# The first four batches of a two-layer graph kernel: loads by other queues, statistics two by two, and two products swapped

## The chip, the cores and the metric

The kernel runs on one core of a Trainium2 chip. The metric is the device time of one execution in microseconds (us). Before the change the median of three runs is 1966.01 us (1965.82 to 1967.39). A core has engines that run side by side, each through its own queue in program order: TensorE (PE, matmuls; PEld in a profile is its loading of the stationary operand), VectorE (DVE), ScalarE (ACT), GpSimd (POOL) and SyncE (SP, here only to issue DMAs). They meet at semaphores.

## The reference

Inputs are x of 128 batches x 128 nodes x 512 features, an adjacency matrix `adj` of 128 x 128, and the weights of one attention layer, all float32. Cut to what matters:

```python
# layer 0: W1 and W2 are both adj, so C - A is the bias b alone
A   = einsum('od,bdn->bon', adj, x)
pre = A[:, :, None, :] + b[None, :, None, None]
x   = layernorm(x + max(relu(pre), axis=-1))      # a single maximum per row of A
# layer 1: masked attention with 8 heads, a projection, its layernorm added
q, k, v = x @ w_qkv
o  = softmax(where(adj == 0, -inf, q @ k.T / 8)) @ v
o  = o @ w_proj + b_proj
x  = layernorm(x + o + layernorm(o) * ln_gamma + ln_beta)
```

So layer 0 needs, for each batch, one 128x128 by 128x512 product with `adj`, the maximum of each of its rows, plus bias, not below zero, added to that row of x, and a layernorm over the 512 features.

## The kernel before

Batches are worked in groups of four. x is loaded in pairs of batches (`load(q)`, lines 103 to 111), either one DMA of 512 KB on SP's queue, or one of 256 KB for each batch on the queues that are given.

A batch f of layer 0 goes through these steps, each a function:

- `l0_mm` (line 282): TensorE multiplies `adjT` with x into a PSUM tile `pa`. A float32 matmul is two instructions.
- `l0_max` (line 286): VectorE takes the row maximum `amax` (line 288) and makes `r` of it with the bias (line 290).
- `l0_add` (line 292): ScalarE adds `r` to x (line 293).
- `bn` (line 247): VectorE takes the statistics (line 249) and aggregates them into a column of `mv` (line 250).
- `finish_stats` (line 252): for all columns of one `mv`, VectorE negates the mean (line 259), and GpSimd adds epsilon (line 261), raises to the power -1/2 and multiplies (line 77). `stats` (line 635) is `bn` for several batches and `finish_stats` behind them.
- `l0_norm` (line 295): ScalarE scales and shifts x (line 275).
- `l0_transpose_pe` (line 314), for the first group only: TensorE transposes x by four 128x128 pieces (line 318), and VectorE copies the result into `x1T` (line 320). Batches f and f + 1 of a pair fill the halves that later products read as one operand of 256 columns.

The products of layer 1 with weights are done by a scheme with seven products in place of eight (`Unit`, lines 163 to 196). A unit works on four batches and a slice of weights. Its products have numbers: `product(1)` and `product(2)` read the first pair's `x1T` and unchanged weights; `product(4)` reads the second pair's `x1T`; products 5, 6, 7 and 3 read sums of the pairs (`left_sums`, made here by VectorE, `run_sums(sums, nc.vector)` on line 708). Products 4, 5, 6, 7 read sums of the weights, which `weight_sums` (line 124) makes on GpSimd: four subtractions for 256 columns. The third and fourth of these depend on the ones before, and product 4 reads the fourth. A product is 8 matmul instructions of 256 columns. Products 1, 6 and 7 share PSUM bank 1; after 1, after 6 and after 7 ScalarE copies that bank to SBUF (`snap`, line 185); 5 and 3 share bank 3.

`keep_warm(n)` (line 85) issues n matmuls of zeros (two instructions each) into a tile that nobody reads.

The order of every engine's instructions is the order in which the program text calls these functions (each is pinned in program order). At the start it is: the adjacency matrix and the bias on SP; pairs 0 and 1 of x, the first batch of each pair on ACT's queue and the second on SP's (lines 137 and 138); a broadcast of beta on ACT; the first 256 columns of the query and key weights by four DMAs on SP, pair 2, the other 256 columns, pair 3. Then the stretch that the diff touches, lines 677 to 716: the four `l0_mm`; for each batch maximum, add and statistics; one `finish_stats` for batches 0 and 1 and one for 2 and 3; both halves of the weight sums; the four norms; ten keep-warm matmuls; the transposes of batches 0 and 1; two keep-warm matmuls. Then unit `cur` begins: product 1, the transposes of batches 2 and 3, product 2, the sums of x, the beta additions and spills of pairs 0 and 1 (GpSimd and SP), products 4, 6 and 5. Batches 4 to 7 of layer 0 follow (`pa` again), and from then on a loop over pairs of batches runs to the end.

Of the kernel before, what the change touches and what calls it, by code (L numbers as in the profile page):

```python
# [9 lines left out]
F32 = mybir.dt.float32  # L10
AF = mybir.ActivationFunctionType
ALU = mybir.AluOpType
# [4 lines left out]
def kernel(  # L17
# [30 lines left out]
    nc = tc.nc  # L48
    B, P, D = x.shape
# [3 lines left out]
    G = 4  # L53
    GT = G * P
    HT = GT // 2
    HE = D // 2
# [10 lines left out]
    small = ctx.enter_context(tc.tile_pool(name="small", bufs=4))  # L67
# [5 lines left out]
    def pe(*args, **kwargs):  # L73
        pin(nc.tensor.matmul(*args, **kwargs))  # L74

    def tt(eng, dst, a, b, op):
        pin(eng.tensor_tensor(dst, a, b, op))  # L77
# [7 lines left out]
    def keep_warm(n):  # L85
        for _ in range(n):
            pe(idle, lhsT=zeros[:, :P], rhs=zeros, start=True, stop=True)
# [6 lines left out]
    def broadcast(queue, name, src):  # L94
        t = const.tile([P, D], F32, name=name)
        pin(queue.dma_start(out=t, in_=src.partition_broadcast(P)))
        return t
# [3 lines left out]
    xs, pairs = {}, {}  # L101

    def load(q, *queues):
        tag, bufs = ("o", 3) if 2 <= q <= 4 else ("x", 2)
        pairs[q] = t = sb.tile([P, 2, D], F32, tag=tag, name=f"x_{q}", bufs=bufs)
        for j, queue in enumerate(queues):
            pin(queue.dma_start(out=t[:, j], in_=x[2 * q + j]))
        if not queues:
            pin(nc.sync.dma_start(out=t, in_=x[ds(2 * q, 2)].rearrange("j p d -> p j d")))
        for j in range(2):  # L110
            xs[2 * q + j] = t[:, j]
# [9 lines left out]
                )  # L121
            )

    def weight_sums(w, cols, width):
        t = w[:, :, :, ds(cols, width)]
        b11, b21, b22, b12 = (t[:, i] for i in range(4))
        tt(nc.gpsimd, t[:, 4], b12, b11, ALU.subtract)
        tt(nc.gpsimd, t[:, 6], b22, b12, ALU.subtract)
        tt(nc.gpsimd, t[:, 5], b22, t[:, 4], ALU.subtract)
        tt(nc.gpsimd, t[:, 3], b21, t[:, 5], ALU.subtract)  # L130

    WQK = [P, 7, 2, D]
    wqk = sb.tile(WQK, F32, tag="wqk", name="wqk")
    wv = const.tile([P, 7, 2, HE], F32, name="wv")
    wp = const.tile([P, 7, 2, HE], F32, name="wp")

    for q in range(2):
        load(q, nc.scalar, nc.sync)
    be_bc = broadcast(nc.scalar, "be_bc", ln_beta)
    weight_load(wqk, w_qkv, 0, D, 0, HE)  # L140
    load(2)
# [102 lines left out]
    NC = 6  # L244
    stat_of = {}

    def bn(src, mv, k):
        st = small.tile([P, 6], F32, tag="st", name=f"st_{k}_{mv.name}")
        pin(nc.vector.bn_stats(st, src))
        pin(nc.vector.bn_aggr(mv[:, k], st))  # L250

    def finish_stats(mv, keys, eng=None, fused=0):

        n = len(keys)
        if n == 0:
            return
        sh = small.tile([P, NC], F32, tag="sh", name=f"sh_{mv.name}")
        if eng is None:
            pin(nc.vector.tensor_scalar(sh[:, :n], mv[:, :n, 0], -1.0, None, ALU.mult))
        rs = small.tile([P, NC], F32, tag="rs", name=f"rs_{mv.name}")  # L260
        pin(nc.gpsimd.tensor_scalar(rs[:, :n], mv[:, :n, 1], EPS, None, ALU.add))  # L261
        tt(nc.gpsimd, rs[:, :n], rs[:, :n], mhalf.to_broadcast([P, n]), ALU.pow)
        if eng is None:
            tt(nc.gpsimd, sh[:, :n], sh[:, :n], rs[:, :n], ALU.mult)
        elif n > fused:

            part = slice(fused, n)
            pin(eng.tensor_scalar(sh[:, part], mv[:, part, 0], -1.0, None, ALU.mult))
            tt(eng, sh[:, part], sh[:, part], rs[:, part], ALU.mult)
        for k, key in enumerate(keys):  # L270
            stat_of[key] = rs[:, k : k + 1], sh[:, k : k + 1]

    def normalize(dst, src, key):
        rs, sh = stat_of.pop(key)
        pin(nc.scalar.activation(dst, src, AF.Identity, bias=sh, scale=rs))  # L275
# [6 lines left out]
    def l0_mm(f, tag="pa"):  # L282
        pas[f] = psum.tile([P, D], F32, tag=tag, name=f"pa_{f}")
        pe(pas[f], lhsT=adjT, rhs=xs[f], start=True, stop=True)

    def l0_max(f):
        amax = small.tile([P, 1], F32, tag="amax", name=f"amax_{f}")
        pin(nc.vector.tensor_reduce(amax, pas.pop(f), AX.X, ALU.max))
        rr[f] = small.tile([P, 1], F32, tag="r", name=f"r_{f}")
        pin(nc.vector.tensor_scalar(rr[f], amax, bias0, 0.0, ALU.add, ALU.max))  # L290

    def l0_add(f):
        pin(nc.scalar.activation(xs[f], xs[f], AF.Identity, bias=rr.pop(f)))

    def l0_norm(f):
        normalize(xs[f], xs[f], ("y", f))

    def x1T_tile(g):
        if g not in x1T:
            x1T[g] = sb.tile([P, 2, KC, 2, Q, QS], F32, tag="x1T", name=f"x1T_{g}", bufs=2)  # L300
        return x1T[g]
# [12 lines left out]
    def l0_transpose_pe(f):  # L314
        g, h, j = place(f)
        ps = psum.tile([P, KC, P], F32, tag=f"pss{j % 2}", name=f"pt_{f}")
        for c in range(KC):
            pin(nc.tensor.transpose(ps[:, c], xs[f][:, ts(c, P)], ident))
        pin(
            nc.vector.tensor_copy(x1T_tile(g)[:, h, :, j].rearrange("p c i b -> p c (i b)"), ps)  # L320
        )
# [35 lines left out]
    def x_sums(g):  # L357
        t = x1T[g].rearrange("p h c j i b -> p h c (j i b)")
        blocks = [t[:, h, ds(2 * d, 2)] for h in range(2) for d in range(2)]
        x_lefts[g], sums = left_sums(f"x_{g}", *blocks)  # L360
        return sums

    def qk_unit(g, q):
        for h in range(2):
            qk[g, q, h] = sb.tile(
                [P, 2, 2, HT], F32, tag=f"qk{h}", name=f"qk_{g}_{q}_{h}", bufs=2 + h
            )
        out = {(h, c): qk[g, q, h][:, c] for h in range(2) for c in range(2)}
        return Unit(f"qk_{g}_{q}", x_lefts[g], weight_stationary(wqk, 2 * q * P), out)
# [13 lines left out]
    def place(b):  # L383
        g, j = divmod(b, G)
        return g, j // 2, j % 2
# [111 lines left out]
    def o_sums(g):  # L497
        blocks = [oT[g, h][:, ds(2 * d, 2)] for h in range(2) for d in range(2)]
        o_lefts[g], sums = left_sums(f"o_{g}", *blocks)
        return sums  # L500
# [134 lines left out]
    def stats(name, *items, eng=None, fused=0):  # L635

        mv = small.tile([P, NC, 2], F32, tag="mv", name=f"mv_{name}")
        for k, (kind, b) in enumerate(items):
            bn({"o": o_of, "z": zs.get, "y": xs.get}[kind](b), mv, k)
        finish_stats(mv, items, eng, fused)  # L640
        return mv
# [33 lines left out]


    for f, tag in enumerate(("pa", "po", "b3", "b4")):
        l0_mm(f, tag)
    mv = [small.tile([P, NC, 2], F32, tag="mv", name=f"mv_first_{k}") for k in range(2)]
    for f in range(G):  # L680
        l0_max(f)
        l0_add(f)
        if f > 0:
            bn(xs[f - 1], mv[(f - 1) // 2], (f - 1) % 2)
        if f == 2:
            finish_stats(mv[0], [("y", 0), ("y", 1)])
    bn(xs[3], mv[1], 1)
    finish_stats(mv[1], [("y", 2), ("y", 3)])
    weight_sums(wqk, 0, HE)
    weight_sums(wqk, HE, HE)  # L690
    for f in range(G):
        l0_norm(f)
    keep_warm(10)
    for f in range(2):
        l0_transpose_pe(f)
    keep_warm(2)


    sums = x_sums(0)
    cur = qk_unit(0, 0)  # L700
# [10 lines left out]
        l0_spill(q)  # L711
    cur.result(0, 0)
    cur.product(4)
    cur.product(6)
    cur.snap(2)
    cur.product(5)
    for f, tag in zip(range(G, 2 * G), ("pa", "po", "pss0", "pss1")):
        l0_mm(f, tag)
    for f in range(G, 2 * G):
# [6 lines left out]
    cur = qk_unit(0, 1)  # L726
# [3 lines left out]
    bp_bc = broadcast(nc.sync, "bp_bc", b_proj)  # L730
    stats("second", *(("y", f) for f in range(G, 2 * G)))
    weight_sums(wv, 0, HE)
    before.snap(3)
    before.result(1, 1)
# [36 lines left out]
    for p in range(LAST + 1):  # L771
# [4 lines left out]
        f = p + 5 if p + 5 < B // 2 else None  # L776
        ta, tb, to = tails(p)
        mv = small.tile([P, NC, 2], F32, tag="mv", name=f"mv_{p}")
# [22 lines left out]
        if ph == 0 and g > 0:  # L801
            sums = o_sums(g - 1)
# [262 lines left out]
    mv = small.tile([P, NC, 2], F32, tag="mv", name="mv_last_4")  # L1065
# [19 lines left out]
    mv = small.tile([P, NC, 2], F32, tag="mv", name="mv_last_5")  # L1085
# [11 lines left out]
    mv = small.tile([P, NC, 2], F32, tag="mv", name="mv_last_6")  # L1097
# [11 lines left out]
    mv = small.tile([P, NC, 2], F32, tag="mv", name="mv_last_7")  # L1109
# [9 lines left out]
    mv = small.tile([P, NC, 2], F32, tag="mv", name="mv_last_8")  # L1119
# [8 lines left out]
    mv = small.tile([P, NC, 2], F32, tag="mv", name="mv_last_9")  # L1128
# [48 lines left out]
```

## Time and profile before

| | us |
|---|---|
| median of three runs | 1966.01 (1965.82 to 1967.39) |
| the profiled execution | 1967.67 |
| its span, first to last instruction | 1965.7 |
| TensorE busy in the span | 1936.3 (99%) |
| VectorE, ScalarE, GpSimd busy | 1560.8, 1062.2, 1296.1 |
| mean granted clock of TensorE | 0.995 |
| first matmul of product 1 starts at | 18.88 |
| first matmul of batch 4 of layer 0 starts at | 29.44 |

Times inside a profile count from the start of the span. A row of the timeline gives start, busy time, engine, line of the program, operation, the tiles written and read, and in brackets how long the engine had been idle and what ended that. Rows that follow one another on an engine are merged, so a row can hold many instructions (x8). Matmuls overlap: a single one takes longer in the row than the distance to the next. "Clock" is the share of TensorE's full speed that was granted.

### The profile page before, as it was taken

The numbers are of one execution on the slowest core, as the hardware profiler recorded it, in microseconds if no ns is written. First come the engines' busy times: TensorE is split into PE (matmuls) and PEld (weight loads), VectorE is DVE, ScalarE is ACT, GpSimd is POOL, SyncE is SP. The second block draws the span as 40 slices with busy tenths as digits, with TensorE's granted clock in tenths as the row PEclk, the third lists the DMA queues.
The fourth block names the chain that finished last, engine by engine and source line by source line (L and its number), as shares of the span: only waits on it lengthen the run. The fifth ranks groups of instructions, "written<-read, shape, count | busy, mean of one in ns | idle before, by whom it ended". The sixth has DMA issues, their size and how long they took to land.

```text
span 1965.7 us, 33048 instructions
## 1 busy us (share of the span) xinstructions
PE 1936.3 (99%) x11543; PEld 1639.7 (83%) x11543; DVE 1560.8 (79%) x2512; ACT 1062.2 (54%) x3084; POOL 1296.1 (66%) x824
## 2 busy tenths in 40 slices
PE   9999999999999999999999999999999999999995
PEld 6888888888888888888888888888888888888883
DVE  6767878778778788787787787887887877877876
ACT  3444655555545546555555455465565555554565
POOL 6336666767667677667676676676676766676748
PEclk9999999999999999999999999999999999999998
DMA  6747576576576676675765755766757667667554
GB/s 216 164 131 182 145 188 173 161 204 162 166 198 160 174 193 159 185 180 161 196 169 164 203 155 169 197 159 180 190 156 191 168 168 201 160 167 199 135 186 141
DMA packets 445654, 341.75 MB, mean 174 GB/s; under 512 B 276912, under 2 KB 378416, under 8 KB 445488
## 3 DMA queue, kind: packets, MB, share of 16 engines
q1 hardware_dynamic: 445056, 338.85, 64.2%
q8 instruction: 92, 1.51, 0.3%
q10 hardware_dynamic: 432, 0.79, 0.1%
q14 instruction: 74, 0.61, 0.1%
HBM read 172.82 MB, written 166.72 MB: 173 GB/s over the span
## 4 chain that ended last, share of the span: by engine, by line
PE 95%; DVE 2%; POOL 1%; DMA 1%; ACT 0%; issue 0%; SPq 0%; POOLq 0%; ACTq 0%; DVEq 0%
PE b_qk L74 39%; PE b_v L74 19%; PE b_o L74 18%; PE pss L74 6%; PE po L74 6%; PE pa L74 6%; POOL zl L77 1%; DMA x<-in_x_dram 0%; DMA wlast<-spill 0%; DVE s L77 0%; POOL rs_mv_last L77 0%; PE idle L74 0%; DVE pu L442 0%; DMA out_dram<-xr 0%; DVE s L402 0%
## 5 line engine op out<-in xcount | busy, mean ns | idle before, releaser
L74 PE MATMUL b_qk<-s_x,wqk 128*128 128x256 f32 x2048 | 473.3, 379 | 1.0 <-DVE s_x L77 0.7
L74 PEld LDWEIGHTS b_qk<-s_x,wqk 128*128 128x128 f32 x2048 | 388.9, 190 | 55.2 <-issue 1.3
L421 ACT ACTIVATE s<-s,nmax 128x128 f32<-128x128 f32 x1024 | 396.1, 391 | 5.7 <-DVE nmax L414 5.7
L74 PE MATMUL b_qk<-x1T,wqk 128*128 128x256 f32 x1536 | 358.7, 383 | 0.1
L74 PEld LDWEIGHTS b_qk<-x1T,wqk 128*128 128x128 f32 x1536 | 286.7, 190 | 45.1 <-issue 1.0
L77 POOL TENSOR_TENSOR z<-z,ga_bc 128x1024 f32<-128x1024 f32 x58 | 164.5, 2836 | 169.3 <-ACT z L275 169.3
L261 POOL TENSOR_SCALAR rs_mv<-mv 128x6 f32<-128x6 f32 (+2 forms) x61 | 14.6, 239 | 381.3 <-DVE mv L250 381.3
L77 DVE TENSOR_TENSOR s<-s,rec 128x1024 f32<-128x1024 f32 x128 | 251.7, 1967 | 4.4
L187 ACT COPY u_qk<-b_qk 128x512 f32<-128x512 f32 x192 | 112.5, 586 | 246.4 <-PE b_qk L74 245.2
L74 PE MATMUL b_v<-wv,s_x 128*128 128x256 f32 x1024 | 236.9, 379 | 0.0
L74 PE MATMUL b_o<-wp,s_o 128*128 128x256 f32 x992 | 231.2, 381 | 3.3 <-POOL s_o L77 2.3
L74 PEld LDWEIGHTS b_v<-wv,s_x 128*128 128x128 f32 x1024 | 194.4, 190 | 26.6
L74 PEld LDWEIGHTS b_o<-wp,s_o 128*128 128x128 f32 x992 | 189.2, 191 | 30.6 <-POOL s_o L77 2.7
L193 DVE TENSOR_TENSOR qk<-b_qk,u_qk 128x512 f32<-128x512 f32 x256 | 168.0, 675 | 57.1 <-PE b_qk L74 44.8
L402 DVE SCALAR_TENSOR_TENSOR s<-pss,mask 128x512 f32<-128x512 f32 x256 | 164.1, 683 | 59.0 <-PE pss L74 58.8
L77 POOL TENSOR_TENSOR x<-x,be_bc 128x1024 f32<-128x1024 f32 x64 | 181.9, 2843 | 33.5 <-DVE rec L432 27.4
L193 DVE TENSOR_TENSOR v<-b_v,u_v 128x512 f32<-128x512 f32 x128 | 87.0, 680 | 137.4 <-PE po L74 132.5
L421 ACT ACTIVATION_READ_ACCUMULATOR s<-s,nmax 128x1 f32 x1024 | 194.4, 190 | 0.0
L187 ACT COPY u_v<-b_v 128x512 f32<-128x512 f32 x96 | 56.2, 586 | 236.7 <-PE b_v L74 236.7
L187 ACT COPY u_o<-b_o 128x512 f32<-128x512 f32 x93 | 54.4, 585 | 237.7 <-PE b_o L74 237.7
L74 PE MATMUL b_v<-wv,x1T 128*128 128x256 f32 x768 | 176.2, 379 | 0.0
L74 PEld LDWEIGHTS b_v<-wv,x1T 128*128 128x128 f32 x768 | 145.9, 190 | 32.2 <-issue 13.9
(121 smaller groups left out, 3396.7 us busy)
## 6 DMA issues: line engine op xcount, KB each, us to landing
hop<-pu SPq DMA_DIRECT2D x128, 512.0 KB, 3.4
pT<-hop SPq DMA_DIRECT2D x512, 128.0 KB, 3.6
spill<-x SPq DMA_DIRECT2D x64, 512.0 KB, 4.8
x<-in_x_dram SPq DMA_DIRECT2D x62, 512.0 KB, 4.3
xhop<-xt SPq DMA_DIRECT2D x248, 128.0 KB, 2.3
x1T<-xhop SPq DMA_DIRECT2D x248, 128.0 KB, 3.9
xr<-spill SPq DMA_DIRECT2D x59, 512.0 KB, 3.2
out_dram<-xr SPq DMA_DIRECT2D x58, 512.0 KB, 4.1
```

Of the source, the lines that this page charges most:

```text
L74: pin(nc.tensor.matmul(*args, **kwargs))
L77: pin(eng.tensor_tensor(dst, a, b, op))
L187: pin(nc.scalar.copy(t, self.banks[1]))
L193: nc.vector.tensor_tensor(self.out[half, col], self.banks[bank], self.snaps[k], ALU.add)
L261: pin(nc.gpsimd.tensor_scalar(rs[:, :n], mv[:, :n, 1], EPS, None, ALU.add))
L402: nc.vector.scalar_tensor_tensor(s[:, par], pss[b][par], SCALE, mask.unsqueeze(1).to_broadcast([P, NP, P]), ALU.mult, ALU.add,)
L421: nc.scalar.activation(prob[b][:, i], prob[b][:, i], AF.Exp, bias=nmax[b][:, i : i + 1], accum_out=psums[b][:, i : i + 1],)
```

## The change

It has four parts. Batches 0 and 1 of x come by ACT's queue, and batches 2 and 3 by SP's. Maximum, add, statistics and norm are done for batches 0 and 1, each with its own statistics, ahead of the maxima of batches 2 and 3; the statistics and norms of batches 2 and 3 stand behind the transposes of batches 0 and 1. The first of the first half's weight sums stands ahead of the statistics of batches 2 and 3, its other three and the second half behind them. The keep-warm matmuls are one before each of the products of batches 2 and 3, three and two, in place of ten and two. In the first unit, product 5 comes ahead of product 6.

```diff
-    def weight_sums(w, cols, width):
+    def weight_sums(w, cols, width, *steps):
         t = w[:, :, :, ds(cols, width)]
         b11, b21, b22, b12 = (t[:, i] for i in range(4))
-        tt(nc.gpsimd, t[:, 4], b12, b11, ALU.subtract)
-        tt(nc.gpsimd, t[:, 6], b22, b12, ALU.subtract)
-        tt(nc.gpsimd, t[:, 5], b22, t[:, 4], ALU.subtract)
-        tt(nc.gpsimd, t[:, 3], b21, t[:, 5], ALU.subtract)
+        sums = ((4, b12, b11), (6, b22, b12), (5, b22, t[:, 4]), (3, b21, t[:, 5]))
+        for i, left, right in {(): sums, (1,): sums[:1], (3,): sums[1:]}[steps]:
+            tt(nc.gpsimd, t[:, i], left, right, ALU.subtract)
...
-    for q in range(2):
-        load(q, nc.scalar, nc.sync)
+    load(0, nc.scalar, nc.scalar)
+    load(1, nc.sync, nc.sync)
...
     for f, tag in enumerate(("pa", "po", "b3", "b4")):
+        keep_warm(f // 2)
         l0_mm(f, tag)
-    mv = [small.tile([P, NC, 2], F32, tag="mv", name=f"mv_first_{k}") for k in range(2)]
-    for f in range(G):
+    for f in range(2):
         l0_max(f)
         l0_add(f)
-        if f > 0:
-            bn(xs[f - 1], mv[(f - 1) // 2], (f - 1) % 2)
-        if f == 2:
-            finish_stats(mv[0], [("y", 0), ("y", 1)])
-    bn(xs[3], mv[1], 1)
-    finish_stats(mv[1], [("y", 2), ("y", 3)])
-    weight_sums(wqk, 0, HE)
-    weight_sums(wqk, HE, HE)
-    for f in range(G):
+    for f in range(2):
+        stats(f"first_{f}", ("y", f))
         l0_norm(f)
-    keep_warm(10)
+    weight_sums(wqk, 0, HE, 1)
+    for f in range(2, G):
+        l0_max(f)
+        l0_add(f)
+    keep_warm(3)
     for f in range(2):
         l0_transpose_pe(f)
+    stats("first_2", ("y", 2), ("y", 3))
+    for f in range(2, G):
+        l0_norm(f)
+    weight_sums(wqk, 0, HE, 3)
+    weight_sums(wqk, HE, HE)
     keep_warm(2)
...
     cur.product(4)
+    cur.product(5)
     cur.product(6)
     cur.snap(2)
-    cur.product(5)
```

## The prediction

> **What bounds the kernel now.** I read the page first, for where TensorE is not busy; then the busy time by stretches, to find which part of the span the change can reach; then the timeline of the first 30 us, the DMA rows of its loads, and the granted clock.
>
> ```profile
> PE 1936.3 (99%) x11543; PEld 1639.7 (83%) x11543; DVE 1560.8 (79%) x2512; ACT 1062.2 (54%) x3084; POOL 1296.1 (66%) x824
> ...
> PE 95%; DVE 2%; POOL 1%; DMA 1%; ACT 0%; issue 0%; SPq 0%; POOLq 0%; ACTq 0%; DVEq 0%
> ```
>
> TensorE (PE) is the bound nearly everywhere, and the chain that ended last is TensorE's for 95%. The busy time by stretches (us, then busy us of PE, PEld, DVE, ACT and POOL, clock, DMA share, GB/s) adds where it isn't:
>
> ```profile
> 0.00:18.88 18.88, 15.21 (x47) 9.65 (x48) 9.01 (x23) 7.39 (x10) 4.62 (x15) 0.91 0.89 291
> 18.88:29.44 10.56, 9.82 (x48) 8.42 (x49) 8.05 (x7) 1.17 (x2) 10.40 (x8) 1.00 0.19 59
> 29.44:80.00 50.56, 50.24 (x267) 40.24 (x267) 36.45 (x67) 23.17 (x59) 25.77 (x22) 1.00 0.83 209
> 80.00:1900.00 1820.00, 1818.97 (x10947) 1552.28 (x10944) 1460.39 (x2335) 996.34 (x2932) 1205.08 (x719) 1.00 0.65 172
> ```
>
> From 29.44 to 1900 us TensorE is idle for 1.35 us in all. So a start that brings the matmuls at 29.44 forward by some time brings the end forward by the same, and one that doesn't brings nothing: the whole change is settled in the first 29 us. In the timeline of TensorE (start, us, engine, line, what, idle before and its releaser) these rows carry it:
>
> ```profile
> 8.16 4.54 PE L74 MATMUL pa<-x,adjT 128*128 128x512 f32 x6 [1.99 <-DMA x<-in_x_dram]
> 12.54 4.48 PE L74 MATMUL idle<-zeros 128*128 128x256 f32 x20
> 16.85 1.04 PE L318 MATMUL pt<-ident,x 128*128 128x128 f32 x8
> 17.73 1.03 PE L74 MATMUL idle<-zeros 128*128 128x256 f32 x4
> 18.88 1.97 PE L74 MATMUL b_qk<-x1T,wqk 128*128 128x256 f32 x8
> 20.68 1.04 PE L318 MATMUL pt<-ident,x 128*128 128x128 f32 x8
> 21.56 3.62 PE L74 MATMUL b_qk<-x1T,wqk 128*128 128x256 f32 x16
> 25.91 3.69 PE L74 MATMUL b_qk<-s_x,wqk 128*128 128x256 f32 x16 [0.74 <-DVE s_x L77]
> 29.44 3.60 PE L74 MATMUL pa<-x,adjT 128*128 128x512 f32 x8
> ```
>
> TensorE waits for batch 1 of x until 8.16, multiplies batches 1 to 3, runs ten keep-warm matmuls, and begins product 1 at 18.88; a product is 8 instructions and takes 1.73 us (3.45 for two in the chain of waits, less the pipeline's end that the rows include). GpSimd's eight weight sums begin only behind the statistics of all four batches:
>
> ```profile
> 17.24 11.33 POOL L77 TENSOR_TENSOR wqk<-wqk 128x512 f32<-128x512 f32 x8
> ```
>
> The loads, by DMA rows in 1.5 to 1.9 us (last column: us from issue to landing):
>
> ```profile
> x<-in_x_dram ACTq DMA_DIRECT2D x1, 256.0 KB, 4.0
> x<-in_x_dram SPq DMA_DIRECT2D x1, 256.0 KB, 6.5
> ```
>
> ACT's second load of x (batch 2, issued at 1.16) lands at 5.2; SP's first (batch 1, issued at 1.64) only at 8.1. And the clock:
>
> ```profile
> 1913.47:1916.88 3.41, 1.29 (x6) 1.16 (x7) 3.34 (x7) 3.41 (x17) 3.33 (x4) 1.00 0.95 384
> 1916.88:1920.30 3.42, 3.42 (x10) 2.39 (x9) 3.32 (x7) 3.03 (x14) 3.34 (x3) 0.50 0.87 219
> 1.99:5.42 3.43, 3.05 (x7) 1.85 (x7) 0.42 (x2) 1.58 (x2) 0.00 (x0) 1.00 0.83 202
> 5.42:8.84 3.42, 1.43 (x4) 0.44 (x3) 0.90 (x2) 0.72 (x1) 0.00 (x0) 1.00 0.85 314
> 8.84:12.25 3.41, 3.41 (x6) 1.35 (x5) 2.51 (x7) 0.72 (x1) 0.00 (x0) 0.50 1.08 369
> ```
>
> A window of 3.41 us in which TensorE was busy for 1.29 or 1.43 us (38% and 42%) is followed by one at half clock; after 3.05 us (89%) the clock is full. A lapse costs up to 1.7 us.
>
> [...] Here the landing does depend on the queue (5.2 against 8.1), since batch 1 stands behind the adjacency and the bias on SP's. [...] a weight sum is 1.27 us alone and 1.61 to 1.72 beside the x sums.
>
> **The change part by part,** first at full clock.
>
> *Loads.* Batch 1 becomes ACT's second load and lands at 5.2; batch 2 becomes SP's first and lands at 8.1; batch 3 and everything queued behind keep their places and sizes (the beta broadcast on ACT, the weights on SP, which wait in order). Batch 1's multiply follows batch 0's directly. If batch 1 landed at 6.6 instead, up to 0.6 us of what follows is lost; I take 5.2, since the same place on the same queue had it.
>
> *First two batches.* Batch 0's maximum starts at 6.21 as before. The second follows at 7.1 (0.69 and 0.21, spaced 0.72 and 0.13); ScalarE's adds (0.72) end at 7.95 and 8.85. VectorE: statistics 0.68, aggregate 0.18, shift 0.17, from 8.0 to 9.1 and again to 10.15. GpSimd per batch: add, power and multiply, spaced 0.32, 0.66 (a one-column power takes 0.58 near the end) and 0.19; from 9.0 to 10.15 and to 11.3. ScalarE's norms (0.80) end at 11.0 and 12.1, against 16.36 (14.86 plus 1.50) before. Splitting the statistics costs two sets of GpSimd instructions in place of one, counted here.
>
> *TensorE up to product 1.* Batch 2 multiplies from 8.16 (0.86), two keep-warm instructions (0.43), batch 3 (0.86), six more (1.3): 11.6. Transposes of batch 0 at 11.6, of batch 1 at 12.15 (0.6 to their end); two copies (0.68) end at 13.45; product 1 starts at 13.55, 5.3 us earlier. Five keep-warm calls fewer are in this.
>
> *What is late next.* Product 2 stands behind the transposes of batches 2 and 3 on TensorE, and these now wait for a longer chain. Their adds stand behind norm 1 on ScalarE (12.1 to 13.55), their statistics behind the copies on VectorE (13.5 to 15.3), then GpSimd (0.32, 0.80, 0.19: to 16.65), norms to 17.5 and 18.2, transposes at 17.5 and 18.2. Product 2 starts at 18.65, 2.9 us earlier.
>
> *Weight sums.* The first fills a hole on GpSimd at 11.3 to 12.55; its weights have landed. The other three follow the statistics: 16.65 plus 5.08 (the first four took 17.24 to 22.32) less 1.24 gives 20.5. Product 4 needs the last: it can start at 20.5 where product 2 ends at 20.4 (23.3 before). The last sum may be slowed beside the x sums by up to 0.45; I take nothing. The second half of the weights ends at about 27, where it ended at 28.6; the beta additions and spills behind it come as much earlier.
>
> *Products 5 and 6.* The x sums start at 19.55; the first is there at 21.0, the second at 22.65. Products 5 and 6 want them at 22.25 and 24.0: no wait, and none in the old order either, so the swap itself is worth nothing here, and 0.74 at most. The next multiplies start at 20.55 + 3 x 1.73 = 25.75 instead of 29.44: 3.7 us saved.
>
> *The clock.* Between product 1's end at 15.3 and the transposes at 17.5 TensorE has nothing, and no keep-warm matmul was put there. With the windows where the profile has them, 15.66 to 19.07 holds 0.9 us of transposes and 0.4 of product 2: 12 to 38%, no more than what brought half clock above. Then 19.07 to 22.49 runs at half: the 1.32 us left of product 2 take 2.64, to 21.7; product 4 gets 0.4 us done by 22.49; the remaining 4.8 us end at 27.3. Of 3.7 us, 2.1 remain; other positions of the window cost 0.9 to 1.7.
>
> *Sum.* The profiled execution took 1967.67 us, 1.97 around its span; less 2.1 it is 1965.6. It stands 1.66 above the median of 1966.01, as much as its half-clock window at 8.84 can explain. If the median run had that lapse, the change gives 1966.01 - 2.1 = 1963.9; if not, 1966.01 + 1.66 - 2.1 = 1965.6. I take the middle, 1964.8.
>
> **The rivals.**
> - *Forecast, 60%: an early start, part of it given back in the gap behind product 1.* 1964.8, its own range 1963.5 to 1966.0.
> - *No lapse in the gap, 22%.* For it: 38% with the transposes counted is close to what is unknown between 42 and 89%, and the window may lie across the gap. Against: product 2 can't fill the gap wherever the window lies. 1966.01 - 3.7 = 1962.3, or 1964.0 over a median without a lapse.
> - *Slower, 12%: the clock lapses twice.* Window 5.42 to 8.84 now holds 2.57 us (75%: 0.6 of batch 0, 0.86, 0.43, 0.68). If the limit lies above 75%, batches 2 and 3 run at half as before, product 1 starts 1.65 later, and the gap's lapse adds 1.6: the next multiplies at 29.0, a gain of 0.4 over the profiled time: 1966.01 + 1.66 - 0.4 = 1967.3. Against it: the window is fuller than before.
> - *Nothing reaches the end, 6%: 1966.0.* A wait past 29.44 takes the gain back. Against it: in that stretch TensorE hardly waits, and what it does wait for shifts along.
>
> **How the numbers follow.** About 0.2% (3.9 us) is what a measurement of this kernel can tell from no change, and the cases lie within it but for one side of the second: below 1962.08 I put two thirds of it (the runs shown spread over 1.6 us) and a little for a chain that I priced too long, 0.17; above 1969.94 half of the third case, should a further lapse or a late load join it, 0.06; the rest, 0.77. The range 1962.3 to 1966.9 takes in the forecast, the second case and the fourth, and leaves most of the third out.
>
> **What would show it.** Right: batch 1's multiply beside batch 0's before 7 us; product 1 at 13.5 to 15; TensorE idle for about 2 us behind it; half clock in a window between 17 and 23; product 4 released by GpSimd's last sum; the pa multiplies of batch 4 at 26 to 28. Wrong: those at 29 or later, or product 1 after 16, or a new wait behind 30 us.

## The result, and the profile after

The changed kernel takes 1964.17 us in the median of 20 runs (1962.92 to 1965.84). The kernel before, now also with 20 runs, takes 1967.02 (1964.33 to 1969.67). The ratio is 0.9986 with a 95% interval of 0.9980 to 0.9993: faster by 0.14%, or 2.85 us between the medians. The median of the three runs shown of before (1966.01) was 1.0 us below that of the 20. The profiled execution took 1965.37 us, with a span of 1963.5 instead of 1965.7. In the changed kernel the lines quoted below that stand behind `weight_sums` have numbers lower by one than before.

The busy time by stretches, after, in the same columns and with the same borders as before:

```profile
0.00:18.88 18.88, 15.06 (x50) 9.29 (x51) 9.20 (x25) 7.60 (x11) 6.76 (x19) 1.00 0.88 292
18.88:29.44 10.56, 10.56 (x44) 7.85 (x44) 10.19 (x12) 1.80 (x4) 10.40 (x7) 1.00 0.17 55
29.44:80.00 50.56, 50.28 (x290) 41.63 (x290) 36.60 (x66) 23.70 (x59) 24.41 (x22) 1.00 0.78 209
80.00:1900.00 1820.00, 1818.96 (x10926) 1552.20 (x10925) 1461.28 (x2335) 997.31 (x2937) 1206.85 (x721) 1.00 0.64 172
```

TensorE is as full from 29.44 on as it was, and it now has no idle time at all from 18.88 to 29.44 (0.74 before). The clock of the first stretch is 1.00 instead of 0.91: the window at half clock behind batch 0 is gone. (The clock column has no entry ahead of the first change. In this execution the first entry, for full clock, is at 6.82, and TensorE was slower up to there: its first four instructions on x, below, take 3.02 us, where number 3 further down needs 1.98.) TensorE's timeline in the first 30 us:

```profile
4.69 3.02 PE L74 MATMUL pa<-x,adjT 128*128 128x512 f32 x4 [0.39 <-DVE adjT L157]
7.55 0.59 PE L74 MATMUL idle<-zeros 128*128 128x256 f32 x2
8.11 1.12 PE L74 MATMUL pa<-x,adjT 128*128 128x512 f32 x2
9.07 0.59 PE L74 MATMUL idle<-zeros 128*128 128x256 f32 x2
9.50 1.02 PE L74 MATMUL pa<-x,adjT 128*128 128x512 f32 x2
10.36 1.46 PE L74 MATMUL idle<-zeros 128*128 128x256 f32 x6
11.65 0.64 PE L317 MATMUL pt<-ident,x 128*128 128x128 f32 x4
12.74 0.66 PE L317 MATMUL pt<-ident,x 128*128 128x128 f32 x4 [0.45 <-ACT x L274]
13.23 1.03 PE L74 MATMUL idle<-zeros 128*128 128x256 f32 x4
14.32 1.99 PE L74 MATMUL b_qk<-x1T,wqk 128*128 128x256 f32 x8
18.02 1.36 PE L317 MATMUL pt<-ident,x 128*128 128x128 f32 x8 [1.71 <-ACT x L274]
19.22 3.75 PE L74 MATMUL b_qk<-x1T,wqk 128*128 128x256 f32 x16
22.80 3.62 PE L74 MATMUL b_qk<-s_x,wqk 128*128 128x256 f32 x16
26.26 3.60 PE L74 MATMUL pa<-x,adjT 128*128 128x512 f32 x8
```

Batch 1 is multiplied directly behind batch 0. Product 1 starts at 14.32, 4.56 us earlier than before; but behind it TensorE idles for 1.71 us for the norm of batch 2 (ScalarE, line 274), so that the multiplies of batch 4 start at 26.26, only 3.18 us earlier. The chain of waits shows what sets the start now (start, us, what):

```profile
14.12 0.61 DVE st_mv_first L248
14.76 0.18 DVE mv_first L249
14.94 0.59 DVE st_mv_first L248
15.55 0.19 DVE mv_first L249
15.82 0.23 POOL rs_mv_first L260
16.14 0.71 POOL rs_mv_first L77
16.93 0.20 POOL sh_mv_first L77
17.15 1.53 ACT x L274 x2
18.73 0.66 PE pt L317 x4
19.38 7.04 PE b_qk L74 x32
```

It is the statistics and norms of batches 2 and 3, which the new order put behind the copies of batches 0 and 1. Of the 3.18 us, 2.2 are left at the end of this execution; where the rest went stands under the tail below.

The measure in what follows is the start of the multiplies of batch 4, since TensorE is full from there on. It can be read to some hundredths in one profile, while the runs of these two kernels spread over 3 and 5 us. But there is one profile of each kernel, and half clock moves the start too: a second profile of the changed kernel (number 9), at half clock from 19.16 to 22.57, has 27.33 instead of 26.26. So the distances from product 1 on are compared only where the clock is known.

### The profile page after: what moved, and what is told of

Same layout as the page of the kernel before. It is cut to its first block, busy times and chain, and to the rows that moved or that the text cites. A ratio compares the mean times of both kernels' runs of the same rounds, so it can differ in the third digit from the quotient of the medians.

```text
span 1963.5 us, 33034 instructions
## 1 busy us (share of the span) xinstructions
PE 1935.3 (99%) x11533; PEld 1637.7 (83%) x11533; DVE 1561.6 (80%) x2513; ACT 1061.6 (54%) x3084; POOL 1297.2 (66%) x827
## 4 chain that ended last, share of the span: by engine, by line
PE 96%; DVE 2%; POOL 1%; ACT 1%; DMA 1%; issue 0%; SPq 0%; POOLq 0%; DVEq 0%; ACTq 0%
PE b_qk L74 40%; PE b_v L74 19%; PE b_o L74 18%; PE pss L74 6%; PE po L74 6%; PE pa L74 5%; PE pp L74 0%; DMA wlast<-spill 0%; ACT s L420 0%; POOL zl L77 0%; DVE s L401 0%; DVE s L77 0%; POOL rs_mv_last L77 0%; DVE st_mv_last L248 0%; DVE pu L441 0%
## 5 line engine op out<-in xcount | busy, mean ns | idle before, releaser
L77 POOL TENSOR_TENSOR x<-x,be_bc 128x1024 f32<-128x1024 f32 x64 | 181.3, 2834 | 33.4 <-DVE rec L431 27.3
```

## The experiments

The theory at the outset: the whole effect lies in the first 29 us, by two means, the chain from the loads to product 4 and lapses of the clock. (A window is a stretch of 3.41 us, as long as the half-clock stretches from 8.84 and from 1916.88 before; the one from 1931.93 after is two of them. A lapse is a window at half clock behind one at full clock, as before behind windows with 1.29 and 1.43 us of TensorE work.) The rivals: the new order of statistics and norms carries it, or the new loads alone do.

**1. The swap undone.**

```diff
     cur.product(4)
-    cur.product(5)
     cur.product(6)
     cur.snap(2)
+    cur.product(5)
```

> The changed kernel with product 6 ahead of product 5 again. Chain theory (the profile after): the second sum of x ends at 23.1 there, and product 6 would want it at 22.6, so TensorE waits about 0.5 us for VectorE and the multiplies of batch 4 start 0.5 later than 26.26. The prediction on record: the swap is worth nothing, no wait, no shift. Median over runs: less than 1 us slower than the changed kernel either way, too small to be told by the times alone.

Measured: 1965.24 us (1964.38 to 1966.82; ratio 0.9988, 0.9981 to 0.9995). In TensorE's timeline of this kernel the wait is back:

```profile
23.01 3.69 PE L74 MATMUL b_qk<-s_x,wqk 128*128 128x256 f32 x16 [0.32 <-DVE s_x L77]
```

From product 1 to the multiplies of batch 4 it takes 12.51 us (14.03 to 26.54), against 11.94 in the changed kernel. No window lapses between these two points in either profile. So the swap is worth 0.57 us, and the prediction's "nothing" was wrong, though within its "0.74 at most".

**2. The loads undone**, the rest of the change kept.

```diff
-    load(0, nc.scalar, nc.scalar)
-    load(1, nc.sync, nc.sync)
+    for q in range(2):
+        load(q, nc.scalar, nc.sync)
```

> The changed kernel with the old queues for the first four batches of x. If the loads carry the gain: batch 1 is multiplied at 8.16 instead of behind batch 0, its norm ends at about 14.2 instead of 12.7, product 1 starts 1.5 us later (15.8) and the multiplies of batch 4 at 27.8 at full clock, later still if the clock lapses in the wait for batch 1; the median rises by 1.5 us or more, to about 1966. If the new order of statistics and norms carries it: the multiplies of batch 4 stay at 26.3 to 26.8 and the median within 0.5 us of the changed kernel.

Measured: 1966.87 us (1965.11 to 1968.87; ratio 0.9995, 0.9987 to 1.0003), no longer told from the kernel before. Product 1 starts at 15.69 and the multiplies of batch 4 at 27.64. Both are where the expectation put them for the case that the loads carry the gain. The 1.8 us that 27.64 is ahead of 29.44 are hardly the new order's: in this profile the window in which TensorE waits for batch 1 (from 5.87) holds 1.85 us of work (54%), and the next, from 9.29, is at full clock. The old order with the clock full at that place starts them at 27.95 (number 6).

**3. The loads alone**, in the kernel before.

```diff
-    for q in range(2):
-        load(q, nc.scalar, nc.sync)
+    load(0, nc.scalar, nc.scalar)
+    load(1, nc.sync, nc.sync)
```

> The kernel before with the new queues for the first four batches of x alone. If the loads carry the gain: batch 1 is multiplied by 7.7, product 1 starts at about 16, the last of the first four weight sums ends at about 20.5 and the multiplies of batch 4 start at 25.8 to 26.3, as early as in the changed kernel although product 1 starts 1.6 us later; median near 1964. If the new order carries it: they start at 28 to 29.4, and the median stays near 1967.

Measured: 1964.44 us (1963.44 to 1966.01; ratio 0.9986, 0.9979 to 0.9993), the same ratio as the whole change. TensorE's timeline of this kernel:

```profile
4.69 1.98 PE L74 MATMUL pa<-x,adjT 128*128 128x512 f32 x4 [0.38 <-DVE adjT L158]
8.18 1.98 PE L74 MATMUL pa<-x,adjT 128*128 128x512 f32 x4 [1.51 <-DMA x<-in_x_dram]
10.01 4.48 PE L74 MATMUL idle<-zeros 128*128 128x256 f32 x20
14.32 1.04 PE L318 MATMUL pt<-ident,x 128*128 128x128 f32 x8
15.20 1.03 PE L74 MATMUL idle<-zeros 128*128 128x256 f32 x4
16.35 1.97 PE L74 MATMUL b_qk<-x1T,wqk 128*128 128x256 f32 x8
18.15 1.04 PE L318 MATMUL pt<-ident,x 128*128 128x128 f32 x8
19.02 3.62 PE L74 MATMUL b_qk<-x1T,wqk 128*128 128x256 f32 x16
22.71 3.69 PE L74 MATMUL b_qk<-s_x,wqk 128*128 128x256 f32 x16
26.23 3.60 PE L74 MATMUL pa<-x,adjT 128*128 128x512 f32 x8
```

Product 1 starts 2.0 us later than in the changed kernel, yet the transposes and product 2 follow it without a gap, and the multiplies of batch 4 start at 26.23 against 26.26. Experiments 2 and 3 together settle it: the loads carry the gain; on the same occasion their medians differ by 2.4 us. The new order brings product 1 forward and pays the same back in the gap behind it. Numbers 1 and 3 show it without the swap: both have the new loads and product 6 ahead of 5, and with the new order product 1 starts 2.3 us earlier, the multiplies of batch 4 0.3 us later, and the median is 0.8 us higher.

**4. The swap alone**, in the kernel before (the diff of the first experiment turned round).

> The kernel before with product 5 ahead of product 6 alone. Chain theory: the wait of 0.74 us for the second sum of x goes, since product 5 wants only the first; from the start of product 1 to that of the multiplies of batch 4 it takes 9.8 us instead of 10.56. Rival: the wait moves to another instruction and the distance stays at 10.5. The median moves by less than 1 us.

Measured: 1966.74 us (1965.86 to 1969.62; ratio 0.9999, 0.9991 to 1.0007), not told from before by its times. From product 1 to the multiplies of batch 4 it takes 9.59 us (18.89 to 28.48) instead of 10.56, so the wait does go, by 0.97 us in this profile.

**5. Keep-warm matmuls behind product 1**, in the changed kernel.

```diff
     cur.product(1)
     cur.snap(1)
+    idle = psum.tile([P, 2 * P], F32, tag="pa", name="idle_gap")
+    keep_warm(4)
```

> The changed kernel with four keep-warm matmuls (1.7 us, into another bank) behind product 1, where TensorE has nothing to do. Theory of the prediction: the clock lapses behind that gap in most runs, 0.9 to 1.7 us each; the median falls by about 1 us. Rival, from the three profiles with this gap, none of which has a lapse there: [...] nothing is won; the multiplies of batch 4 stay at 26.3 and the median within 0.5 us of the changed kernel.

Measured: 1963.78 us (1963.39 to 1965.31; ratio 0.9984, 0.9976 to 0.9991). The median is 0.4 us below the changed kernel's, which its spread doesn't tell from nothing: so far the expectation that nothing is won holds. The multiplies of batch 4 start at 25.73, but the filled gap is not why: the first four instructions on x take 2.22 us here instead of 3.02, product 1 starts at 13.69, and from there it takes 12.04 us, against 11.94 in the changed kernel, whose first profile has no lapse behind product 1. Its gap is divided between two windows, with 2.62 and 2.40 us of work, and the one behind them, from 20.47, is at full clock too (the clock stands ahead of the DMA share):

```profile
13.64:17.05 3.41, 2.62 (x11) 1.63 (x10) 2.19 (x6) 0.27 (x1) 1.06 (x3) 1.00 1.07 370
17.05:20.47 3.42, 2.40 (x14) 2.03 (x15) 1.71 (x3) 1.99 (x3) 3.34 (x4) 1.00 1.01 333
```

In number 1 most of the gap lies in one window, and the next, from 19.72, is still at full clock. Of its 1.93 us, 1.31 are transposes:

```profile
16.31:19.72 3.41, 1.93 (x12) 1.62 (x13) 1.27 (x2) 1.99 (x3) 3.25 (x5) 1.00 1.08 362
```

What the gap can cost is seen in two other executions that have it, below (7 and 9).

**6. Keep-warm matmuls in the wait for batch 1**, in the kernel before.

```diff
     for f, tag in enumerate(("pa", "po", "b3", "b4")):
+        if f == 1:
+            keep_warm(3)
         l0_mm(f, tag)
```

> The kernel before with three keep-warm matmuls between the multiplies of batch 0 and batch 1, where TensorE waits for the load. If half of what the new loads bring is the clock: the window behind stays at full clock, the multiplies of batch 4 start at 27.8 instead of 29.44 (new loads alone: 26.23), and the median falls by 1 us or more, to about 1966. If all of it is the earlier data: they stay at 29.4, and the median near 1967.5.

Measured: 1965.94 us (1965.17 to 1967.09; ratio 0.9994, 0.9987 to 1.0000). Two windows of this kernel:

```profile
4.94:8.35 3.41, 2.35 (x9) 1.37 (x9) 0.91 (x2) 0.72 (x1) 0.00 (x0) 1.00 0.79 288
8.35:11.76 3.41, 3.41 (x10) 1.90 (x11) 2.25 (x5) 0.72 (x1) 0.00 (x0) 1.00 1.09 374
```

Behind 2.35 us busy instead of 1.43, the next window is at full clock, and the multiplies of batch 4 start at 27.95 instead of 29.44. So in the profiles the gain of the loads (29.44 to 26.23) splits into 1.5 us of clock and 1.7 us of earlier data. By the medians, each against the kernel before on its own occasion, it is 1.3 of 3.1 us. The runs spread over 1.9 us instead of some 5, which fits with a lapse that comes in some runs and not in others.

**7. Keep-warm matmuls in the tail** of the changed kernel.

```diff
     attend(L - 1)
+    idle = psum.tile([P, 2 * P], F32, tag="pss1", name="idle_end")
+    keep_warm(6)
     attend(L, "pa")
```

> The changed kernel with six keep-warm matmuls (2.6 us) near the end, between the attention products of the last two batches, where TensorE waits 3.7 us for a DMA and two windows at half clock followed in the profile. If the tail's lapses explain why 3.2 us won at the start were 2.2 at the end of the profile: the projections behind (24 instructions) take 10.6 us instead of 12.7, the median falls by 1 to 2 us to about 1963, and the spread narrows. Rival: the wait for that DMA sets the end alone; the median stays at 1964.2.

Measured: 1964.20 us (1962.72 to 1965.22; ratio 0.9985, 0.9977 to 0.9992). In the changed kernel's profile the windows at this place are

```profile
1928.52:1931.93 3.41, 0.21 (x4) 0.00 (x0) 2.75 (x5) 2.17 (x5) 2.92 (x7) 1.00 0.85 240
1931.93:1935.35 3.42, 2.89 (x17) 2.10 (x18) 1.30 (x2) 2.33 (x5) 3.01 (x7) 0.50 0.38 144
1935.35:1938.76 3.41, 3.41 (x5) 1.35 (x4) 1.72 (x5) 1.82 (x3) 3.25 (x3) 0.50 0.41 154
```

and the 24 projections behind take 12.74 us; with the keep-warm matmuls they take 10.57, as long as at full clock in the profile before (from 1936.72), and as expected. From the multiplies of batch 4 to the end of the span it was 1936.26 us before, 1937.24 in the changed kernel and 1934.82 here. At the product that starts at 1906.47 (1909.69 before) the changed kernel's profile was still 3.2 us ahead, so the 1.0 us that it lost lies behind that, in the tail: these two windows at half clock cost 2.2 us of the projections' time, and the execution of before had lost one window, at 1916.88. With the two gone, the chain of waits that ends last is mostly GpSimd's from 1924 on.

But the median didn't move, which was not expected. The changed kernel's second profile (number 9) gives one reason: it needs 1935.77 us for the same stretch without any keep-warm matmuls there, so that 1.5 of the 2.4 us between 1937.24 and 1934.82 were an unlucky tail in the first. Another is that three of the 15 runs here, the profiled one among them, have 2.7 to 3.2 us outside of the span, where the others have about 2: by the spans alone the median is 1961.8, against 1962.25 in the changed kernel, a difference that the spread doesn't tell from nothing either. This profile also has the very lapse behind product 1 that the prediction named:

```profile
14.80:18.21 3.41, 1.53 (x9) 0.86 (x8) 0.57 (x4) 1.69 (x3) 2.85 (x5) 1.00 1.06 376
18.21:21.62 3.41, 3.41 (x11) 2.87 (x12) 2.93 (x4) 0.30 (x1) 3.33 (x3) 0.50 0.71 226
```

The multiplies of batch 4 start at 27.18 here, 13.58 us behind product 1, against 11.94 in the changed kernel's first profile.

**8. A candidate:** the kernel before with the new loads, the swap, the first weight sum ahead of the second pair's statistics (as a call of its own behind the first `finish_stats`), and the tail's keep-warm matmuls.

> A candidate: the kernel before with the new loads, product 5 ahead of product 6, the first weight sum ahead of the second pair's statistics, and the tail's keep-warm matmuls; neither the new order of statistics and norms nor the other keep-warm matmuls. If the loads carry the change: the multiplies of batch 4 start at 26.0 (26.23 with the loads alone, less the wait for the second sum of x), and with the tail it is as fast as the changed kernel with the tail's keep-warm matmuls, or faster: median about 1963. If the new order is worth something: about 1 us slower than that.

Measured: 1963.46 us (1962.73 to 1964.13; ratio 0.9979, 0.9971 to 0.9988). The multiplies of batch 4 start at 25.85; the chain from product 1 takes 9.58 us, as with the swap alone, so the early weight sum adds nothing there.

**9 to 11. The changed kernel again, and two candidates, on one chip.** Number 10 is number 8 without the tail's keep-warm matmuls; number 11 is the changed kernel with those of numbers 5 and 7.

> The changed kernel again, beside the two candidates on one chip and as a second look at the phase of its windows: median 1964.2, the multiplies of batch 4 at 25.7 to 26.3 where no window lapses behind product 1, and at about 27.2 where one does.

> The kernel before with the new loads, product 5 ahead of product 6 and the first weight sum ahead of the second pair's statistics, without keep-warm matmuls in the tail. If the tail's matmuls are worth nothing in the median (as e7 against the changed kernel): about 1963.5, as e8. If they are what made e8 fast: about 1964.4, as the loads alone. The multiplies of batch 4 start at 25.9 either way.

> The changed kernel with keep-warm matmuls both behind product 1 and in the tail. If the lapses of both gaps cost independently: no window of the first 30 us lapses, the projections in the tail take 10.6 us, and the median is about 1963, 1 us below the changed kernel's and with a narrower spread. If the tail's matmuls win nothing: 1963.8, as with the first gap alone.

Measured: the changed kernel again 1964.35 us (1963.18 to 1966.26), number 10 1963.96 (1962.68 to 1965.00), number 11 1963.49 (1962.80 to 1964.26); ratios 0.9989, 0.9985 and 0.9983. The changed kernel's profile lapses behind product 1 this time:

```profile
15.74:19.16 3.42, 1.57 (x10) 1.30 (x11) 0.92 (x2) 1.99 (x3) 3.26 (x4) 1.00 1.07 370
19.16:22.57 3.41, 3.41 (x9) 2.70 (x8) 3.34 (x4) 0.00 (x0) 3.41 (x3) 0.50 0.43 137
```

Its multiplies of batch 4 start at 27.33, 13.59 us behind product 1: the lapse costs 1.6 us. Those of number 11, whose gap is filled, start at 25.51, and no row from the multiplies of batch 0 to there shows a lapse: its first four instructions on x take 1.98 us, and products 2 and 4 take 3.76 instead of 5.30 in number 9. Numbers 10 and 11 each lie between their two expected medians (1963.5 and 1964.4; 1963 and 1963.8) and decide neither question. With the gap filled, the tail's matmuls lower the median by 0.3 us (11 against 5); beside the loads, the swap and the first sum by 0.5 (8 against 10); in the changed kernel itself by nothing (0.4 by the spans). Each of these pairs ran on different occasions, and half a microsecond between medians is at the edge of what they tell. Numbers 8 and 11 have the lowest medians and spread over 1.4 and 1.5 us, where the changed kernel spreads over 2.9: they beat both kernels by their medians, though their intervals overlap with the changed kernel's.

## Why the prediction was right, and where it was not

- *Where the effect lies.* Right. In all 13 profiles TensorE is busy for 1859.6 to 1859.8 of the 1860 us from 30 to 1890, so what tells the kernels apart lies in the first 30 us and in the tail.
- *The loads.* Right: ACT's second load lands 4.2 us after its issue at 1.16, 5.4 against 5.2.
- *The first two batches and product 1.* 14.32 instead of 13.55. Batch 0's maximum started at 6.81 and not at 6.21, since in this execution the first four instructions on x took 3.02 us, and all behind it moved with it. In the execution of number 11, where they took 1.98, product 1 started at 13.46.
- *What is late next, and the weight sums.* Right in kind: product 2 waits for the norms (19.22 against 18.65), and product 4 follows it as the last sum ends (its weight load starts at 20.97, after 0.26 us of waiting for GpSimd).
- *The swap.* Wrong: "no wait, and none in the old order either". The working had the second sum at 22.65 and product 6 in the old order at 22.25, so the 0.4 us stood there and was overlooked. Undone, it costs 0.57.
- *The multiplies of batch 4 at full clock.* 25.75 predicted, 12.2 us behind product 1; 26.26 here, 11.94 behind it.
- *The clock behind product 1.* Its price was right: with a lapse, 27.3 was predicted, and 27.18 and 27.33 were measured. So was the lapse that it foresaw for a window from 15.66 to 19.07: in number 9 the window lies there (15.74 to 19.16), holds 46% instead of 12 to 38% (the author's estimate, without the transposes and with them), and half clock follows. What failed is that no position was taken to escape ("other positions of the window cost 0.9 to 1.7", "product 2 can't fill the gap wherever the window lies"). Of the five profiles with this gap open (the changed kernel twice, numbers 1, 2 and 7) three don't lapse. In the changed kernel's first the gap is divided between two windows (77% and 70%); in number 2 the window that holds it has 1.70 us of work (50%), most of it product 1; in number 1 it holds 57%, transposes counted. Whether the 60% for a lapse were too high, five profiles can't tell.
- *The sum.* Predicted 1964.8, measured 1964.17, and in part by luck. The forecast was a gain of 1.2 us from a base of 1966.01; the measured gain is 2.85, from a base that lies 1.0 higher over 20 runs, and the two errors partly cancel. The term that was mis-sized is the middle between a median with the first lapse (a gain of 2.1) and one without it (0.4). The gain of 2.85 lies between 2.1 and the 3.7 without a lapse behind product 1, which fits with that lapse in a part of the runs. But the first lapse and the tail vary as well, and the second rival's 1964.0 is as near as the forecast's 1963.9, so the median doesn't tell the two apart. The profiles show both: the forecast's lapse in two of five, the second rival in the changed kernel's own first profile.
- *The other rivals.* The third needed half clock behind a window with 75%; in number 7 one with 2.42 us (71%, from 4.56) was followed by full clock. The fourth, that nothing reaches the end, is ruled out by the interval of the ratio.
- *What the prediction didn't see* is that most of the change isn't needed. It priced the parts along one path and never asked what the loads would do in the old order. There batches 2 and 3 have their statistics early, and the gap behind product 1 doesn't come about.

Left open: whether the early weight sum and the tail's keep-warm matmuls are worth anything of their own in the median, and in what share of the runs each lapse occurs.

## What to carry to other kernels

Where one engine is full from some point on, price a change at that point and not at the first instruction that it brings forward: 4.56 us at product 1 were 3.18 at the first place without a wait behind it. When a change has several parts, work out each of them alone too; here the two lines that choose the queues of the first four batches did as much as all of it. And count the clock: here the window with a wait of 1.99 us held 1.43 us of work and was followed by half clock, and with three matmuls of zeros in the wait the next window was at full clock and the multiplies of batch 4 started 1.5 us earlier (29.44 against 27.95, number 6).

## What the runs showed of the hardware that was not expected

*Full clock behind little work.* In the profile before, half clock followed windows with 1.29 us (38%) and 1.43 us of work (42%). In the tail of the changed kernel full clock followed one with 1.51 us (44%):

```profile
1945.59:1949.00 3.41, 1.51 (x4) 0.38 (x2) 2.46 (x7) 0.00 (x0) 3.08 (x5) 1.00 0.31 112
1949.00:1952.41 3.41, 0.00 (x0) 0.00 (x0) 3.27 (x8) 2.22 (x3) 3.25 (x4) 1.00 0.20 76
```

These are the profile's busy times, in which the ends of matmuls are modelled, and no more than three windows.

*Half clock behind more work.* Behind a window at half clock with 2.89 us of work (85%, from 1931.93 in the changed kernel) the next was at half clock again. In the same execution full clock followed one with 3.04 us (89%, from 3.40, before the first entry of the clock).

*Windows with transposes.* Full clock followed the window of number 1 above, of whose 1.93 us all but 0.6 (18% of the window) are transposes. Half clock followed the two behind product 1 with 1.53 us (number 7, about half of it transposes) and 1.57 us (number 9, most of it transposes), though both hold more than the 1.51 us above. What the transposes have to do with it was not shown: the difference is some hundredths of a microsecond.

*Two profiles of one kernel.* The two profiles of the changed kernel differ by 1.07 us at the multiplies of batch 4 (26.26 and 27.33), and by 0.4 us the other way in their spans (1963.5 and 1963.1). Only the second lapses behind product 1. In the tail the first is at half clock from 1931.93 to 1938.76. In the second other rows are long: the 24 products of `b_o` from 1913.49 take 7.13 us, where the first, from 1912.70, needs 6.02 with a wait of 0.31. The two were taken on different occasions.
